# A four-layer sequence kernel: the expert group of four tiles placed second, the second chunk's first norms and sums on VectorE, and a new order table

## The chip, the core and the metric

The kernel runs on one core of one Trainium2 chip. The metric is the device time of one execution in microseconds (us). The kernel before was timed in nine runs: median 668.4, from 666.0 to 671.02.

A core has TensorE (PE in the profile; its weight loads are PEld), VectorE (DVE), ScalarE (ACT), GpSimd (POOL) and SyncE (SP, which only issues transfers). They run side by side and wait for each other through semaphores. Each engine works through its own queue strictly in order, so an instruction that waits holds up all that is queued behind it on its engine.

## The reference

The input is 8 sequences of 512 steps with 128 features, all float32. Four layers follow each other, each with a residual sum and a layer norm in front:

```python
x = x + ssm(layernorm(x))          # gated linear recurrence over the steps, both
                                   # outer weights divided by max(largest singular value, 1)
x = x + layernorm(x) @ W[idx] + b[idx]       # idx: argmax of logits + gumbel noise
x = x + delta(layernorm(x))        # 16 heads of 8; per step, with normalised k:
    # S = S + beta * (v - S k) k^T ;  o = S q        then  x + scan_out @ w_out + b_out
x = x + experts(layernorm(x))      # softmax router, the best 2 of 8 experts per token:
    # h = gelu(x w1[e]) (128 -> 512) ;  y = h w2[e] (512 -> 128) ;  weighted sum of the two
```

The third layer's state S of each sequence and head goes from step to step, so it is a chain over 512 steps.

## The kernel before

**Tiles and chunks.** A tile is 16 steps of all 8 sequences, 128 tokens. There are 32 tiles. They are worked in chunks of `SIZES` = 2, 4, 4, 4, 4, 4, 4, 4, 2 tiles; `FROM[g]` is a chunk's first tile. For each chunk the kernel runs `first_layers` (the first two layers: `scanned`, `ssm_out`, `linear`), then `delta_in` (projections, key norms and the 4x4 block matrices `tmat` of the delta rule), then `delta_rule`, then `route`.

**The recurrence.** `delta_rule` takes four steps at a time: each tile has 4 blocks, 128 in all. A block is six VectorE instructions, each of which needs the one before: a reduction of the last state product (`st<-so`), `prod<-tmat,st`, a reduction, `st<-kq,st`, a reduction, and the state product `so<-kq,st`. The last of these is called the state product below. GpSimd, TensorE and ScalarE turn the products of a tile into its output x3.

**The experts.** `route` norms x3, finds the two best experts and their weights, and appends its chunk to the open group. `GROUPS` (line 28) says which chunks share a group; when a group's last chunk is routed, `experts` is recorded for the whole group. It computes a place in a table in DRAM for each (token, expert) pair, such that each block of 128 rows belongs to one expert. GpSimd sends each tile's rows there with two indirect transfers (`scatter`, "places<-xne" in the profile, two for a tile). Then, block by block, SP loads the rows and the block's expert weights `w1b` (256 KB), TensorE transposes the rows, multiplies by w1 (`ph`), ScalarE takes the GELU (`hid`), TensorE multiplies by w2, and the results go to DRAM. Behind a group's last block GpSimd fetches the rows back (`back<-results`, again two for a tile), and they are weighted and summed into `fin` and written out. A group of n tiles has (2*128*n - 8)//128 + 8 blocks. The last chunk, of two tiles, is not sorted: `every_expert` runs all eight experts over it (called dense here).

**The start.** The largest singular value of two weight matrices comes from 21 squarings of each on TensorE, with copies on VectorE; at its end stands `gain`, which the first layer's output needs. The products of the expert weights with `less_last` (`kq<-in`) are spread in between.

**Who norms.** `factors` makes the scale and shift of a norm, `normalised` applies it tile by tile. With `leads` true the shift is one VectorE instruction and the norm a VectorE instruction for each tile; otherwise the shift is two GpSimd instructions and the norm a ScalarE instruction for each tile. `leads` is `g == 0`, the first chunk. In the same way `ssm_out` and `linear` sum on VectorE for the first chunk and for late chunks, and otherwise let TensorE add the residual through a product with the identity and ScalarE copy the sum.

**What sets the order.** Nothing is issued directly. A `Recorder` for each engine records every instruction into a `Plan` with its operands, a cost and a due time (`nc.key`, from `due(tile)` = 15 a tile). `Plan.ordered` then emits the recorded instructions in the order of the number table `ORDER` (line 383), and gives the PSUM banks from the string `BANKS` (line 630); both were made beforehand from the planner's own costs. So the position of each instruction in its engine's queue is written out by hand, as it were, in that table. As one helper issues all of them, nearly all lines of the profile name L330; groups are told apart by the names of their tiles.

**Lines the change touches:** 28 (`GROUPS`), 75 and 300 (`Plan`), 374 (`PRESUM` and the constants behind it), 383 (`ORDER`), 630 (`BANKS`), and in `seq_kernel` the functions `input_statistics`, `scanned`, `ssm_out`, `linear` and `scatter`.

Of the kernel before, what the change touches and what calls it, by code (L numbers as in the profile page):

```python
# [27 lines left out]
GROUPS = ((2,), (4, 4), (4, 4), (4, 4), (4,), (2,))  # L28
# [41 lines left out]
class Plan:  # L70
# [4 lines left out]
    def __init__(self, tc, banks):  # L75
        self.tc, self.hw, self.banks = tc, tc.nc, banks
        self.ops, self.seen, self.key, self.slack = [], {}, 0.0, 0.0
        self.tensor, self.vector, self.scalar, self.gpsimd, self.sync = (
            Recorder(self, e) for e in ("tensor", "vector", "scalar", "gpsimd", "sync")
        )  # L80
# [213 lines left out]
    def emit(self):  # L294
        kind = mybir.EngineType
        with self.tc.manual_schedule(engines={kind.PE, kind.DVE, kind.Activation, kind.SP}):
            for op, switch in self.best():
                if switch:
                    self.hw.scalar.preload_act_table_set(switch)  # L299
                made = op.emit()  # L300
                if op.engine == "gpsimd":
                    self.tc.keep_in_program_order(made)
# [51 lines left out]
def _cost(engine, name, n, kw):  # L354
# [16 lines left out]
TENSOR_SUMS = 12  # L371
PERIOD = 15.0
BEHIND = 8.0
BURST, WINDOW = 4, 6.0
LAG = {"tensor": 0.4, "vector": 0.3, "scalar": 0.3, "gpsimd": 0.3, "sync": 0.3}
# [8 lines left out]
    3, 10, 38, 43, 36, 37, 45, 35, 34, 48, 44, 1, 5, 53, 0, 9, 50, 49, 57, 46, 7, 335, 52, 8, 11, 32, 51, 47, 33, 4,  # L384
    12, 59, 126, 39, 61, 58, 31, 2, 13, 6, 16, 14, 327, 67, 62, 15, 40, 129, 63, 17, 64, 54, 130, 65, 18, 131, 336,
    66, 19, 343, 132, 21, 323, 133, 435, 55, 134, 324, 830, 135, 68, 153, 70, 145, 154, 328, 69, 146, 106, 444, 160,
    101, 107, 100, 325, 77, 152, 42, 147, 163, 60, 108, 326, 102, 155, 161, 390, 103, 391, 104, 392, 337, 148, 393,
    109, 344, 338, 156, 110, 112, 71, 149, 394, 87, 111, 41, 150, 98, 136, 157, 113, 151, 339, 367, 399, 158, 114,
    162, 340, 418, 137, 351, 159, 72, 165, 164, 400, 329, 375, 167, 341, 401, 330, 56, 397, 359, 405, 115, 74, 166,
    128, 395, 331, 116, 168, 406, 117, 22, 342, 332, 118, 176, 105, 170, 407, 119, 398, 169, 29, 171, 182, 175, 185,  # L390
    120, 333, 172, 138, 183, 173, 73, 174, 184, 334, 396, 187, 408, 402, 423, 188, 177, 409, 191, 139, 178, 403, 80,
    197, 179, 180, 181, 140, 99, 186, 141, 205, 346, 142, 192, 189, 410, 193, 404, 190, 345, 198, 199, 411, 194, 81,
    195, 200, 196, 204, 347, 206, 207, 201, 202, 209, 422, 203, 143, 412, 208, 210, 211, 348, 413, 213, 212, 214,
    219, 414, 446, 220, 215, 221, 226, 445, 222, 216, 349, 90, 415, 23, 223, 217, 224, 416, 218, 225, 417, 227, 447,
    229, 420, 228, 91, 231, 448, 419, 449, 424, 450, 230, 232, 144, 233, 421, 425, 236, 451, 235, 360, 237, 452, 241,
    427, 383, 238, 453, 249, 239, 234, 352, 240, 121, 243, 368, 250, 428, 458, 27, 20, 350, 253, 242, 460, 244, 254,
    429, 248, 258, 257, 245, 246, 251, 459, 247, 259, 263, 252, 271, 464, 260, 255, 261, 262, 272, 465, 256, 275,
    265, 454, 466, 276, 280, 281, 264, 455, 307, 426, 266, 282, 122, 279, 283, 270, 267, 284, 273, 268, 285, 269,
    293, 481, 274, 309, 277, 294, 297, 278, 286, 287, 298, 288, 301, 456, 292, 467, 289, 290, 291, 295, 362, 302,
    457, 361, 303, 468, 296, 461, 299, 88, 354, 300, 462, 353, 304, 384, 89, 469, 305, 25, 363, 313, 306, 355, 312,  # L400
    92, 376, 315, 463, 316, 24, 317, 318, 319, 320, 93, 470, 321, 364, 356, 430, 84, 322, 641, 431, 127, 432, 78,
    433, 28, 85, 434, 314, 365, 436, 30, 477, 437, 311, 471, 310, 308, 438, 79, 439, 440, 385, 94, 472, 123, 473, 95,
    124, 644, 82, 96, 125, 643, 645, 474, 441, 83, 442, 642, 475, 443, 499, 86, 482, 357, 358, 515, 517, 487, 516,
    518, 476, 519, 369, 522, 386, 521, 479, 523, 1065, 524, 478, 483, 520, 646, 525, 647, 484, 648, 649, 480, 783,
    650, 740, 377, 526, 378, 485, 527, 370, 486, 528, 379, 371, 655, 677, 488, 657, 489, 372, 490, 380, 373, 491,
    492, 656, 494, 651, 493, 387, 661, 388, 389, 653, 495, 662, 496, 652, 663, 366, 497, 664, 529, 97, 654, 26, 665,
    509, 659, 498, 658, 530, 666, 531, 660, 532, 500, 667, 501, 533, 502, 504, 534, 505, 503, 506, 535, 507, 1066,
    536, 508, 668, 381, 537, 548, 374, 547, 510, 538, 545, 511, 1068, 512, 546, 549, 669, 539, 513, 550, 540, 514,
    543, 695, 551, 541, 711, 552, 575, 1069, 576, 573, 670, 544, 578, 577, 554, 712, 574, 542, 714, 579, 553, 580,
    555, 558, 678, 671, 586, 581, 560, 382, 559, 557, 562, 672, 561, 563, 556, 582, 564, 673, 565, 592, 566, 583,  # L410
    567, 675, 568, 584, 569, 593, 585, 715, 594, 713, 595, 588, 674, 679, 596, 716, 590, 717, 597, 676, 589, 718,
    754, 680, 599, 587, 600, 719, 755, 682, 598, 720, 605, 601, 721, 681, 722, 591, 723, 602, 683, 724, 606, 725,
    603, 570, 614, 726, 1067, 684, 604, 571, 727, 685, 572, 728, 686, 729, 1070, 687, 619, 613, 730, 1071, 1413, 688,
    1072, 731, 1073, 607, 689, 617, 1074, 732, 690, 611, 733, 608, 734, 753, 735, 618, 691, 609, 615, 736, 692, 738,
    737, 610, 620, 739, 625, 757, 1136, 741, 616, 693, 758, 621, 694, 759, 696, 760, 622, 626, 697, 761, 612, 742,
    627, 699, 743, 1137, 762, 1079, 698, 629, 1135, 756, 623, 763, 624, 744, 628, 764, 1081, 745, 765, 1075, 766,
    1080, 630, 767, 1085, 746, 768, 1077, 631, 1086, 769, 1076, 1087, 747, 770, 771, 748, 772, 749, 632, 773, 1088,
    774, 700, 633, 701, 1078, 775, 702, 634, 703, 750, 1089, 776, 705, 777, 635, 778, 779, 636, 780, 781, 637, 1416,
    1138, 1090, 784, 1178, 1082, 751, 1139, 785, 752, 1140, 786, 1179, 1141, 1415, 1083, 787, 704, 1142, 1177, 1164,
    788, 1414, 1143, 706, 1417, 789, 707, 1084, 1144, 790, 708, 1145, 709, 1146, 1418, 1091, 1147, 791, 710, 1419,  # L420
    1148, 1102, 1149, 1150, 1420, 782, 999, 1092, 1151, 1000, 1152, 1119, 792, 1153, 1093, 793, 1154, 794, 1155,
# [217 lines left out]
def seq_kernel(  # L639
# [459 lines left out]
    def tiles_of(v):  # L1099
        return [v[:, i, :] for i in range(v.shape[1])]  # L1100
# [31 lines left out]
    def input_statistics(g, x):  # L1132
        of_input[g] = factors(moments(x, "i", 3), "i", 1, g == 0, NG)
# [887 lines left out]
```

## Time and profile before

| what | us |
|---|---|
| median of nine runs | 668.4 |
| the profiled execution | 670.72 |
| its span, first to last instruction | 669.0 |
| TensorE busy (80% of the span) | 532.7 |
| ScalarE busy (70%) | 468.8 |
| VectorE busy (69%) | 463.0 |
| GpSimd busy (69%) | 458.8 |
| end of the gain's computation on ScalarE | 51.4 |
| first block of the recurrence begins | 91.5 |
| last state product of tile 29 ends | 501.8 |
| last state product of tile 31 ends | 546.2 |
| last matmul ends | 662.9 |

Of the groups, these matter here (mean duration of one):

| group | count | mean ns |
|---|---|---|
| VectorE, six instructions of a block | 128 each | 491, 284, 291, 426, 497, 685 |
| GpSimd, rows to places | 60 | 1000 |
| GpSimd, rows back from results | 60 | 979 |
| ScalarE, table load | 64 | 1283 |
| ScalarE, GELU 128x512 | 111 | 597 |

A row of the profile has the line, engine and operation, then the tile written, an arrow, the tiles read, their shapes, the start and the duration, and in brackets how long the engine had been idle and who released it. TensorE's instructions are counted in passes: one float32 product shows as two. Some matmul records are missing from a trace, a few per cent.

### The profile page before, as it was taken

The numbers are of one execution on the slowest core, as the hardware profiler recorded it, in microseconds if no ns is written. First come the engines' busy times: TensorE is split into PE (matmuls) and PEld (weight loads), VectorE is DVE, ScalarE is ACT, GpSimd is POOL, SyncE is SP. The second block draws the span as 40 slices with busy tenths as digits, with TensorE's granted clock in tenths as the row PEclk, the third lists the DMA queues.
The fourth block names the chain that finished last, engine by engine and source line by source line (L and its number), as shares of the span: only waits on it lengthen the run. The fifth ranks groups of instructions, "written<-read, shape, count | busy, mean of one in ns | idle before, by whom it ended". The sixth has DMA issues, their size and how long they took to land.

```text
span 669.0 us, 10937 instructions
## 1 busy us (share of the span) xinstructions
PE 532.7 (80%) x3077; PEld 416.0 (62%) x3077; DVE 463.0 (69%) x1290; ACT 468.8 (70%) x984; POOL 458.8 (69%) x603
## 2 busy tenths in 40 slices
PE   3886668687796688796998787998978998778876
PEld 3653234454554455673676575787868987668775
DVE  7567158999988999989899998998971950002021
ACT  2875887879768579988999997857765553536421
POOL 6545467768768748899987978886589668454340
PEclk9898778989779789989999897999989988998988
DMA  4938145236243556446775585888887775665531
GB/s 133 326 116 271 59 107 148 68 80 157 64 126 77 167 138 181 135 123 193 198 196 155 146 218 151 232 224 202 217 218 230 220 228 191 188 211 186 168 106 35
DMA packets 96721, 110.16 MB, mean 165 GB/s; under 512 B 10179, under 2 KB 68206, under 8 KB 96662
## 3 DMA queue, kind: packets, MB, share of 16 engines
q1 hardware_dynamic: 91984, 101.31, 54.3%
q0 software_dynamic: 3904, 8.00, 4.4%
q8 instruction: 26, 0.43, 0.3%
q14 instruction: 33, 0.27, 0.1%
q10 hardware_dynamic: 774, 0.15, 0.1%
HBM read 85.90 MB, written 27.48 MB: 169 GB/s over the span
## 4 chain that ended last, share of the span: by engine, by line
DVE 34%; PE 30%; ACT 13%; POOL 9%; issue 5%; DMA 3%; another core or an unknown queue 3%; ACTq 1%; SPq 1%; DVEq 0%; POOLq 0%
DVE st L330 16%; PE in L330 11%; PE ph L330 9%; DVE so L330 7%; PE po L330 5%; POOL places L1685 4%; PE po L1747 4%; ACT f L330 3%; DVE prod L330 3%; ACT hid L330 2%; PE in L1747 2%; ACT L299 2%; ACT b L330 2%; POOL so L330 1%
## 5 line engine op out<-in xcount | busy, mean ns | idle before, releaser
L330 PE MATMUL ph<-xbT,w1b 128*128 128x128 f32 x760 | 142.6, 289 | 12.3 <-ACT hid L330 6.2
L330 PEld LDWEIGHTS ph<-xbT,w1b 128*128 128x128 f32 x760 | 115.0, 201 | 19.2 <-ACT hid L330 8.2
L330 ACT ACTIVATE hid<-ph 128x512 f32<-128x512 f32 x111 | 65.5, 597 | 86.6 <-PE ph L330 47.0
L1747 PE MATMUL po<-w_sb,hid 128*128 x536 | 105.5, 288 | 4.3 <-ACT hid L330 3.5
L1747 PEld LDWEIGHTS po<-w_sb,hid 128*128 128x128 f32 x536 | 85.6, 202 | 14.5 <-issue 8.4
L330 DVE TENSOR_TENSOR so<-kq,st 128x512 f32<-128x512 f32 x128 | 87.6, 685 | 5.8 <-PE in L330 0.6
L299 ACT ACT_TABLE_LOAD x64 | 82.1, 1283 | 9.2 <-DMA hid<-in_L_attn_ln_b_dram 8.1
L1685 POOL DMA_INDIRECT places<-xne,small_dest x60 | 60.0, 1000 | 20.7 <-issue 10.5
L330 POOL DMA_INDIRECT back<-results,small_dest x60 | 58.7, 979 | 21.3 <-issue 14.1
L330 DVE TENSOR_REDUCE st<-st 128x64 f32<-128x320 f32 x128 | 63.6, 497 | 3.7
L330 DVE TENSOR_REDUCE st<-so 128x32 f32<-128x320 f32 x128 | 62.8, 491 | 3.9 <-ACT so L330 0.8
L330 DVE TENSOR_TENSOR st<-kq,st 128x256 f32<-128x256 f32 x128 | 54.5, 426 | 3.5
L330 PE MATMUL po<-wo,so 128*128 128x128 f32 x240 | 48.6, 306 | 8.9 <-POOL so L330 6.6
L330 PEld LDWEIGHTS po<-wo,so 128*128 128x128 f32 x240 | 40.7, 215 | 23.9 <-POOL so L330 9.4
L330 PE MATMUL in<-b,wqkvb 128*128 128x512 f32 (+1 forms) x72 | 39.7, 641 | 11.5 <-ACT b L330 3.6
L1747 PE MATMUL in<-w_sb,hid 128*128 x224 | 45.6, 288 | 1.8 <-issue 1.3
L330 PE MATMUL in<-f,wT 128*128 128x512 f32 (+1 forms) x72 | 40.1, 650 | 8.1 <-DVE small_best L330 3.7
L330 DVE TENSOR_TENSOR prod<-tmat,st 128x128 f32<-128x128 f32 x128 | 36.4, 284 | 7.4 <-POOL tmat L330 4.2
L330 POOL TENSOR_TENSOR f<-f,f 128x512 f32<-128x512 f32 (+1 forms) x27 | 32.4, 1201 | 12.7 <-ACT f L330 12.5
L330 DVE TENSOR_REDUCE st<-prod 128x32 f32<-128x128 f32 x128 | 37.2, 291 | 5.6 <-ACT upd L330 1.0
L330 POOL TENSOR_TENSOR fin<-fin,back 128x512 f32<-128x512 f32 (+1 forms) x14 | 16.7, 1196 | 32.9 <-ACT back L330 32.7
L330 PE MATMUL ph<-ident,xb 128*128 128x128 f32 x95 | 28.3, 306 | 13.4 <-ACT hid L330 11.3
(339 smaller groups left out, 1389.6 us busy)
## 6 DMA issues: line engine op xcount, KB each, us to landing
kq<-scratch SPq DMA_DIRECT2D x64, 512.0 KB
w1b<-w1b_dram SPq DMA_DIRECT2D x103, 256.0 KB
xb<-places SPq DMA_DIRECT2D x20, 256.0 KB
results<-yb SPq DMA_DIRECT2D x20, 256.0 KB
places<-yb SPq DMA_DIRECT2D x2, 1472.0 KB
kq<-in_L_ffn_w_dram SPq DMA_DIRECT2D x2, 1024.0 KB
w1b_dram<-kq SPq DMA_DIRECT2D x2, 1024.0 KB
u_rows<-in_L_attn_u_dram SPq DMA_DIRECT2D x7, 256.0 KB
```

The lines of the kernel that those rows point to most:

```text
L299: self.hw.scalar.preload_act_table_set(switch)
L330: return method(*(on(x) for x in args), **{k: on(x) for k, x in kw.items()})
L1685: rows_out = hw.gpsimd.indirect_dma_start(out=table[0 : nblk * P, :], out_offset=bass.IndirectOffsetOnAxis(ap=at, axis=0), in_=src, in_off ...
L1747: return hw.tensor.matmul(out_.on(nc.banks), lhsT=src, rhs=w2_f[:, bass.ds(at + c * P, P)], start=(c == 0), stop=(c == NHB - 1),)
```

## The change

Three things, and a fourth that the numbers leave without effect:

1. The groups are 2; 4; 4, 4; 4, 4; 4, 4; 2 tiles and not 2; 4, 4; 4, 4; 4, 4; 4; 2. The chunk sizes stay. The group of four tiles is now tiles 2 to 5; the last recorded group is tiles 22 to 29, where it was 26 to 29.
2. The second chunk (four tiles) is led as the first: its first and second norms' shifts and norms and its two residual sums go to VectorE. The transposed input of both chunks is copied out of PSUM by VectorE.
3. `ORDER` and `BANKS` are new throughout.
4. The plan can make a row transfer wait for an earlier one when `ROW` of them stand in a row without a longer GpSimd instruction between them; `ROW` is 99.

```diff
-GROUPS = ((2,), (4, 4), (4, 4), (4, 4), (4,), (2,))
+GROUPS = ((2,), (4,), (4, 4), (4, 4), (4, 4), (2,))
...
+                self.to_land = self.row[-1] if op.by_rows and len(self.row) == ROW else None
                 made = op.emit()
-                if op.engine == "gpsimd":
-                    self.tc.keep_in_program_order(made)
+                if op.engine != "gpsimd":
+                    continue
+                self.tc.keep_in_program_order(made)
+                if self.to_land:
+                    wait = mybir.DependencyInfo(mybir.DependencyClass.Sync, mybir.DependencyReason.DATA)
+                    self.tc.add_manual_dep(made.ins, self.to_land, wait, reason="short rows of indirect transfers")
+                    self.row = []
+                if op.by_rows:
+                    self.row.append(made.ins.name)
+                elif op.cost > 0.6:
+                    self.row = []
...
+LEADS = 2
 BURST, WINDOW = 4, 6.0
+ROW = 99
...
 ORDER = (
...
 BANKS = (
...
     def input_statistics(g, x):
-        of_input[g] = factors(moments(x, "i", 3), "i", 1, g == 0, NG)
+        of_input[g] = factors(moments(x, "i", 3), "i", 1, g < LEADS, NG)
...
-        nc.scalar.copy(xT, transposed(normalised(x, rstd, shift, tiles_of(xn.rearrange("p (i d) -> p i d", d=D)), leads=g == 0)))
+        copied = nc.vector.tensor_copy if g < LEADS else nc.scalar.copy
+        copied(xT, transposed(normalised(x, rstd, shift, tiles_of(xn.rearrange("p (i d) -> p i d", d=D)), leads=g < LEADS)))
...
     def ssm_out(x, r, g):
-        if g == 0 or FROM[g] > TENSOR_SUMS:
+        if g < LEADS or FROM[g] > TENSOR_SUMS:
             nc.vector.scalar_tensor_tensor(x1, tokens_out(r, wT[:, 4, :]), gain, x, ALU.mult, ALU.add)
...
     def linear(x1, g):
-        leads = g == 0
+        leads = g < LEADS
...
-        if g == 0 or FROM[g] > TENSOR_SUMS:
+        if g < LEADS or FROM[g] > TENSOR_SUMS:
             nc.vector.tensor_add(x2, tokens_out(xT, wsel), x1)
...
                 for before_ in scattered:
-                    tc.declare_no_dep(rows_out.ins, before_, reason="every row has places of its own")
+                    if before_ != nc.to_land:
+                        tc.declare_no_dep(rows_out.ins, before_, reason="every row has places of its own")
```

One rule of `experts` depends on a group's last tile: where the group ends at tile 28 or later, its rows are weighted and summed by VectorE multiply-adds, one for each tile and expert (now two chunks, before one), and otherwise by ScalarE multiplications and GpSimd sums.

## Prediction

> **What bounds the kernel now.** I read the page's slices first, then a table of stretches cut at the stage limits, then VectorE's timeline around the recurrence's end, then ScalarE's and VectorE's timelines of the start. The slices (40, of 16.7 us) show three stages.
>
> ```profile
> PE   3886668687796688796998787998978998778876
> DVE  7567158999988999989899998998971950002021
> ACT  2875887879768579988999997857765553536421
> POOL 6545467768768748899987978886589668454340
> ```
>
> A start of five slices in which no engine is full all through; a middle, to about 500 us, in which VectorE is at 9; and a tail in which VectorE is idle and TensorE is the fullest. The second view is the table of stretches (start:end, length, busy us and instruction counts of TensorE, weight loads, VectorE, ScalarE, GpSimd, then TensorE's clock, DMA share, GB/s). I cut at the gain's arrival (51.4), the first recurrence block (91.5), the end of tile 29 (501.8), the last state product (546.2) and the last matmul (662.9).
>
> ```profile
> 0.00:51.40 51.40, 36.48 (x157) 26.74 (x157) 33.78 (x154) 32.19 (x92) 26.81 (x64) 0.93 0.62 191
> 51.40:91.50 40.10, 27.09 (x74) 14.67 (x74) 14.73 (x29) 29.59 (x66) 22.15 (x37) 0.75 0.48 153
> 91.50:501.80 410.30, 332.58 (x1853) 247.72 (x1852) 374.14 (x983) 332.62 (x675) 322.40 (x405) 0.91 0.60 158
> 501.80:546.20 44.40, 40.02 (x305) 37.65 (x305) 24.84 (x78) 23.43 (x52) 34.81 (x44) 0.92 0.79 224
> 546.20:662.90 116.70, 96.52 (x694) 89.16 (x693) 14.86 (x49) 50.98 (x103) 52.67 (x55) 0.94 0.55 166
> 662.90:669.00 6.10, 0.00 (x0) 0.00 (x0) 0.61 (x2) 0.00 (x0) 0.00 (x0) 0.72 0.08 22
> ```
>
> VectorE works 374 of 410 us in the middle. From 501.8 to 662.9, 161.1 us, TensorE works 136.5 us and is idle 24.6. So the time is start + VectorE's middle + TensorE's tail. Third, VectorE as tile 30 begins:
>
> ```profile
> 501.91 0.49 DVE L330 TENSOR_REDUCE st<-so 128x32 f32<-128x320 f32 x1
> 508.22 0.29 DVE L330 TENSOR_TENSOR x<-po,base 128x128 f32<-128x128 f32 x1 [5.81 <-PE po L330]
> ...
> 514.11 0.69 DVE L330 TENSOR_TENSOR acc<-po,x 128x512 f32<-128x512 f32 x1 [0.99 <-issue]
> 518.59 0.29 DVE L330 TENSOR_TENSOR prod<-tmat,st 128x128 f32<-128x128 f32 x1 [3.79 <-POOL tmat L330]
> ```
>
> The recurrence stands still from 502.4 to 518.6, because the block matrices (tmat) of the last chunk come from GpSimd, which was sending 16 row scatters. TensorE meanwhile was 90% busy, so this hole looks large and costs little.
>
> **The expert group moved.** A group of n tiles has (2·128n - 8)//128 + 8 blocks: 11, 15 and 23 for 2, 4 and 8 tiles. Six groups give 95 routed blocks before and after; no matmul goes away there. I counted the order tables behind the last state product of tile 29: 521 matmuls and transposes before, 524 after. Behind that of tile 31: 357 before, 413 after. So the last recorded group grows from 15 blocks to 23, but the plan has the same TensorE work left at the end of tile 29. What differs is where the recurrence stands: in the new order the last chunk's tmat is written at tile 29.25, before tile 30 needs it, where it stood at 29.75 behind the last of the scatters. The 16.2 us hole goes, and tiles 30 and 31 should take about 2 x 14.5 us (their VectorE rows sum to 29.0) and not 44.4. TensorE then has 56 more instructions after the recurrence, 56 x 2 passes x 0.131 us (40.02/305, the saturated stretch) = 14.7 us. Gain 15.4, loss 14.7: nothing is won by the hole itself. That is the main step of this forecast.
>
> Two things are late next. The last group's 16 scatters: the order has them from tile 31.25 on, with 427 TensorE instructions left at the first and 342 at the last, and the first of its transposes at 317. Their spacing in the trace was 1.4 us (550.89, 552.31, 553.76, 555.23): 22.7 us for 16, which 85 x 2 x 0.131 = 22.3 us of TensorE work covers. Then the landing, 5.2 us, and the block load, 3.0 us in the chain of waits; 25 instructions cover 6.6 of these 8.2. And the gathers behind the last block: 16 where there were 8, with 8 more VectorE multiply-adds (0.35 us each) in place of 8 ScalarE multiplications and 2 GpSimd additions. Gathers followed each other by 1.25 us (636.34 to 645.21): 10 us more. Before, the last block's copy ended at 632.2, the gathers began at 636.3, the last multiply-add ended at 651.1. After: 632.2 + 4.1 + 20.1 + 4.9 = 661.3 on the old scale, then two output hops begun 2.3 us apart, some 5 us: 666. The old end was 669, through the dense experts, so this stays hidden by 3 us. If that cover is gone it costs what it exceeds.
>
> **The start.** ScalarE loses 12 instructions of the second chunk: eight norms at 0.49, three copies of 512 at 0.59 and the first chunk's 0.36 copy, 6.0 us. TensorE loses two products with the identity. VectorE gets 8 norms (0.35), copies and sums of 0.68 to 0.74, two shifts at 0.16, GpSimd loses four small ones at 0.2. VectorE is busy only 14.7 of 40.1 us there, which is the cover; without it the price would be about 6 us. One wait is new: the second chunk's x2 sum (0.68) with its two moments (0.42 each) stands in VectorE's queue between block 0's first reduction and the first chunk's tmat; all of block 0 is queued behind it. Before, the two moments alone stood in front of that reduction; I count the 0.7 us in the lower bound below. Between the gain and the copy that lets block 0 begin, ScalarE's queue holds 64 instructions, 34.8 us with two table loads, before, and 50, 27.5 us, after; the copy stood at 91.25. The timeline shows what is in front of the first chunk's keys:
>
> ```profile
> 67.57 0.56 ACT L330 ACTIVATE b<-in,cols 128x256 f32<-128x256 f32 x1 [0.78 <-PE in L330]
> ...
> 74.60 1.28 ACT L299 ACT_TABLE_LOAD   x1
> ...
> 77.88 1.28 ACT L299 ACT_TABLE_LOAD   x1
> ...
> 79.81 0.46 ACT L330 ACTIVATE knq<-in,cols 128x256 f32<-128x256 f32 x1
> ```
>
> Seventeen instructions of 10.9 us stand between b and knq, eight of 7.0 us in the new order. Upper bound of the gain: 7.3 us. Lower bound below nothing: two more weight products and ten more VectorE instructions (3.6 us) now stand ahead of the gain; TensorE was 95% busy from 30 to 40 us, and if nothing of the 7.3 is won and most of this delays the squarings, the start is 3 us later. I take 4 us earlier, nearer the upper end, because VectorE was idle 17.6 of the first 51.4 us.
>
> The norms have one bad price in the trace:
>
> ```profile
> 61.58 0.33 DVE L330 TENSOR_SCALAR b<-x,small_rstdb,small_shiftb 128x128 f32<-128x128 f32 x1
> 61.83 2.51 DVE L330 TENSOR_SCALAR base<-x,small_rstdb,small_shiftb 128x128 f32<-128x128 f32 x2
> ```
>
> The same instruction takes 0.33 us and, beside GpSimd's two products of 1.30 and 1.26 us from 61.72 on, 1.26 each. Eight norms lie between 8 x 0.35 = 2.8 and 8 x 1.29 = 10.3 us; I take the lower, as four stand ahead of the gain, where GpSimd is busy 26.8 of 51.4 us, and the rest has 25 us of idle VectorE.
>
> The Trainium skill, "SBUF — State Buffer", Who interferes with whom, has the rule behind this row and against this part of the change: a VectorE tensor_scalar in a two-port mode and a GpSimd instruction take a shared port pair in turn, and the second blocks fully. By the rule the worst case is the 10.3 us, by the low row 2.8; GpSimd would be held up by the same ports.
>
> In the middle, from block 0 to the end of tile 29, VectorE's rows sum to 392.2 us in the old order and 393.3 in the new: +1.1. Table loads fall from 64 to 56, 8 x 1.28 = 10.3 us of ScalarE, which is not the bound there; in the tail a load delays a GELU that TensorE waits for. The Trainium skill, "ScalarE: Activation LUTs", What ACT_TABLE_LOAD costs, prices a switch at 2.66 us with its drain; here the next instruction starts 1.30 us after the load does (74.60, 75.90), and by the page's price the eight would be 21 us.
>
> SP's 338 recorded transfers stay 338: each block takes its weight load and row loads along, and DMA engines at 0.55 to 0.79 in the tail have room for six to eight blocks more behind 546. The code for rows (ROW = 99) does nothing: no run of row transfers reaches 99.
>
> **Sum.** End of tile 29: 501.8 - 4 + 1.1 = 498.9. TensorE's tail: 161.1 x 524/521 = 162.0, less 3 of the 24.6 idle us for loads and for scatter waits that a deeper store of blocks covers (bounds: 0 and 14, the idle beyond 9% as at 501.8 to 546.2). Then 6.1 us of output. 664.0 of span, 5.0 less than 669.0. The profiled execution took 670.7, 0.3% over the median of 668.4; I put the difference to the median: 663.4 us.
>
> **Rivals.** *Scatters too late* (slower). With groups of eight tiles the way from the last tile's end to the first product of its rows took 69.5 us before (tile 25 ends at 446.4, blocks of it at 515.95). The new order hopes for some 54 (30 for tile 30 and 31, 16 of scatters left, 8 of landing). With L us of it the end is T29 + L + 317 x 0.309 (161.1/521 per instruction) + 6.1; it decides from L = 61. At 69.5: 498.9 + 69.5 + 98.0 + 6.1 = 672.5, and 675.6 where the start brings 1 us: some 674, or 673.4 as a time. For: GpSimd's rows behind the recurrence sum to 59.7 us, and the block load has 1.6 us less cover than it takes; against: the blocks of the group before cover.
> *Nothing moves.* The start's 4 us are lost in the middle, where the second and third chunks wait for GpSimd (80% busy): 669, time 668.4. For: tile 0 took 20.0 us (91.5 to 111.5), VectorE idle for 3.7 of them.
> *A full tail.* With 56 more instructions stored TensorE keeps the pace of 501.8 to 546.2 (44.4 us for 164 instructions, 0.271): 498.9 + 142.0 + 6.1 = 647. I take half of the way from 664, 655.5, as GELU waits came back in every slice after 546: time 655.
>
> **How the numbers follow.** Forecast 0.38, scatters too late 0.31, nothing 0.17, full tail 0.14. 0.3% (2 us) is about what this measurement tells from no change. Faster by more: the full tail, most of the forecast (0.33), little of nothing moves (0.03), 0.50; slower: the late scatters (0.30) and a part of nothing moves (0.06), 0.36; the same 0.14. The forecast's own range is 658 to 669; 8 in 10 reach from 651 to 679, the late scatters with a start 3 us later.
>
> **What would show it.** Right: block 0 before 89 us; no wait of VectorE over 4 us at tile 30, the last state product near 528; TensorE over 87% busy from there to its end; tmat of the last chunk ahead of the scatters. Wrong: TensorE idle over 4 us before the last group's first transposes (late scatters); the gain after 54 us; a last multiply-add of the gathered rows behind the last dense product.

## The result, and the profile after

The changed kernel takes 684.85 us (median of 20 runs, 675.65 to 689.86) against 667.13 us (62 runs of the kernel before on the same chips): a ratio of 1.0237, with a 95% interval of 1.0211 to 1.0264. The change costs 2.4%, where 0.7% of gain was forecast, and the time lies above the predicted range. Medians here are of all runs, ratios of the fast ones alone (six of the 20 runs of the changed kernel count as slow), so that this ratio is below the quotient of the medians, 1.0265.

The profiled execution took 682.29 us, 680.6 of them the span. Its first lines and the slices (40, of 17.0 us; busy tenths):

```profile
span 680.6 us, 10891 instructions
...
PE 530.6 (78%) x3073; PEld 415.2 (61%) x3073; DVE 477.7 (70%) x1312; ACT 453.8 (67%) x956; POOL 454.4 (67%) x597
...
PE   3986868668586788888878878994977968979964
...
DVE  7685459899999999989998898996797800001112
```

TensorE's busy time is about what it was (530.6 us, before 532.7), so the 11.6 us that the span grew are TensorE standing idle. VectorE is busy to slice 32, with dips to 6 and 7 in slices 28 and 29; the hole of the old kernel, the 1 in its slice 31, is gone.

The table of stretches, cut at the same events as in the prediction (start:end, length, busy us and counts of TensorE, weight loads, VectorE, ScalarE, GpSimd, then TensorE's clock, DMA share, GB/s): the gain's arrival, block 0, the end of tile 29, the last state product, the last matmul.

```profile
0.00:52.00 52.00, 37.58 (x155) 27.28 (x155) 40.23 (x155) 27.40 (x76) 26.02 (x64) 0.93 0.56 168
52.00:90.90 38.90, 27.78 (x68) 13.27 (x68) 16.61 (x39) 27.01 (x61) 18.61 (x25) 0.69 0.50 166
90.90:511.80 420.90, 329.67 (x1857) 250.88 (x1857) 380.60 (x986) 327.28 (x677) 327.68 (x423) 0.91 0.59 157
511.80:545.60 33.80, 29.47 (x217) 27.25 (x216) 26.84 (x82) 19.09 (x38) 22.68 (x26) 0.90 0.68 191
545.60:674.00 128.40, 106.08 (x785) 96.47 (x783) 13.46 (x53) 53.02 (x105) 59.42 (x62) 0.97 0.58 170
674.00:680.60 6.60, 0.00 (x0) 0.00 (x0) 0.00 (x0) 0.00 (x0) 0.00 (x0) 0.77 0.27 61
```

(The first cut is at 52.0; the gain itself came at 57.5. The last is at 674.0; the last matmul ended at 673.0.) Set against the rows before, TensorE's idle time is length minus busy: 14.9 and 13.0 us in the two stretches of the start before, 14.4 and 11.1 now; 77.7 before and **91.2** now in the middle; 4.4 and 4.3 in the stretch of tiles 30 and 31; 20.2 and 21.3 in the tail, up to the last matmul. So 13.5 us of idle time are new in the middle, before any of the work that the change moved to the end begins. From the end of tile 29 on, TensorE has 1002 records left and the kernel needs 168.8 us; before it was 999 records and 167.2 us.

The same in phases of the recurrence, by which the experiments are compared below (us, one execution each):

| | start to tile 0's end | tiles 1-26 | 27-29 | 30, 31 | rest | span |
|---|---|---|---|---|---|---|
| before | 111.5 | 349.3 | 40.9 | 44.4 | 122.8 | 669.0 |
| after | 113.5 | 352.2 | 46.1 | 33.9 | 135.0 | 680.6 |

The hole of tile 30 did close: 10.5 us. The rest behind the recurrence grew by 12.2. And tiles 27 to 29 hold a new hole. VectorE's timeline at tile 27 of the changed kernel (start, us, engine, line, operation, tiles and shapes, idle time before and who ended it):

```profile
470.62 0.43 DVE L341 TENSOR_TENSOR st<-kq,st 128x256 f32<-128x256 f32 x1
480.49 0.29 DVE L341 TENSOR_TENSOR x<-po,base 128x128 f32<-128x128 f32 x1 [9.45 <-PE po L341]
480.70 0.49 DVE L341 TENSOR_REDUCE st<-st 128x64 f32<-128x320 f32 x1
```

The recurrence stands in the middle of a block for 9.45 us, because a residual sum (`x<-po`) stands in VectorE's queue and waits for TensorE. What TensorE waited for is in its own timeline, and what that waited for is in GpSimd's:

```profile
475.66 0.80 PE L341 MATMUL po<-wo,so 128*128 128x128 f32 x2 [6.84 <-POOL so L341]
```

```profile
460.65 0.26 POOL L341 TENSOR_TENSOR small_both<-small_mine 128x32 f32<-128x32 f32 x1
461.07 0.99 POOL L1699 DMA_INDIRECT places<-xne,small_dest  x1 [0.17 <-issue]
462.37 0.96 POOL L1699 DMA_INDIRECT places<-xne,small_dest  x1 [0.30 <-issue]
...
472.48 0.96 POOL L1699 DMA_INDIRECT places<-xne,small_dest  x1 [0.30 <-issue]
473.47 0.92 POOL L341 TENSOR_TENSOR qkp<-qkp,upd 128x384 f32<-128x384 f32 x1
474.34 1.26 POOL L341 TENSOR_TENSOR so<-so 128x512 f32<-128x512 f32 x1
```

Ten scatters follow each other, one each 1.27 us, and the two sums for the attention output (`qkp`, `so`) of tile 26 come behind all of them. In the order table they stand behind the second of the ten. The table isn't what runs: the plan pins each GpSimd instruction behind the one issued before it, but a scatter declares that it depends on no earlier scatter of its group, and with that declaration the pin between two scatters goes as well. A scatter whose predecessor in the table is a scatter may then go ahead of other work. Compared place by place with the queue of the same kernel with its scatters pinned (experiments 11 and 1 below), 30 of GpSimd's 603 instructions are others in the kernel before, and 45 of 597 in the changed one.

### The profile page after: what moved, and what is told of

It is laid out like the page before. It is cut to its first block, busy times and chain, and to the rows that moved or that the text cites. A ratio compares the mean times of both kernels' runs of the same rounds, so it can differ in the third digit from the quotient of the medians.

```text
span 680.6 us, 10891 instructions
## 1 busy us (share of the span) xinstructions
PE 530.6 (78%) x3073; PEld 415.2 (61%) x3073; DVE 477.7 (70%) x1312; ACT 453.8 (67%) x956; POOL 454.4 (67%) x597
## 4 chain that ended last, share of the span: by engine, by line
DVE 35%; PE 25%; POOL 14%; ACT 12%; issue 9%; another core or an unknown queue 2%; DMA 2%; DVEq 0%; POOLq 0%; ACTq 0%
DVE st L341 16%; PE in L341 9%; PE ph L341 6%; DVE so L341 6%; PE po L341 6%; POOL places L1699 5%; ACT f L341 4%; DVE prod L341 3%; PE po L1762 2%; ACT L300 2%; POOL so L341 2%; POOL back L341 1%; ACT b L341 1%; ACT hid L341 1%
## 5 line engine op out<-in xcount | busy, mean ns | idle before, releaser
L341 PE MATMUL ph<-xbT,w1b 128*128 128x128 f32 x760 | 141.2, 290 | 21.3 <-ACT hid L341 15.5
L341 PEld LDWEIGHTS ph<-xbT,w1b 128*128 128x128 f32 x760 | 114.8, 202 | 33.8 <-ACT hid L341 18.0
L1762 PE MATMUL po<-w_sb,hid 128*128 x496 | 96.2, 283 | 3.4 <-DVE so L341 2.3
L1762 PEld LDWEIGHTS po<-w_sb,hid 128*128 128x128 f32 x496 | 77.6, 197 | 10.1 <-issue 8.1
L1699 POOL DMA_INDIRECT places<-xne,small_dest x60 | 60.6, 1011 | 16.3 <-issue 12.2
L341 PE MATMUL po<-wo,so 128*128 128x128 f32 x248 | 50.0, 316 | 16.8 <-POOL so L341 12.2
L1762 PE MATMUL in<-w_sb,hid 128*128 x264 | 55.5, 300 | 4.9 <-DVE acc L341 2.7
L341 PEld LDWEIGHTS po<-wo,so 128*128 128x128 f32 x248 | 42.5, 224 | 26.9 <-POOL so L341 14.1
L341 DVE TENSOR_TENSOR st<-kq,st 128x256 f32<-128x256 f32 x128 | 54.5, 426 | 3.5
L1762 PEld LDWEIGHTS in<-w_sb,hid 128*128 128x128 f32 x264 | 43.7, 209 | 9.3 <-DVE acc L341 2.9
L341 PE MATMUL in<-f,wT 128*128 128x512 f32 (+1 forms) x72 | 41.7, 667 | 8.9 <-ACT f L341 6.9
L341 POOL TENSOR_TENSOR qkp<-qkp,upd 128x384 f32<-128x384 f32 x32 | 29.2, 913 | 21.3 <-ACT upd L341 18.5
L341 POOL TENSOR_TENSOR f<-f,f 128x512 f32<-128x512 f32 (+1 forms) x27 | 31.1, 1153 | 17.0 <-ACT f L341 16.8
```

The source lines that it names most:

```text
L341: return method(*(on(x) for x in args), **{k: on(x) for k, x in kw.items()})
L1699: rows_out = hw.gpsimd.indirect_dma_start(out=table[0 : nblk * P, :], out_offset=bass.IndirectOffsetOnAxis(ap=at, axis=0), in_=src, in_off ...
L1762: return hw.tensor.matmul(out_.on(nc.banks), lhsT=src, rhs=w2_f[:, bass.ds(at + c * P, P)], start=(c == 0), stop=(c == NHB - 1),)
```

## The experiments

The kernel before was timed beside each experiment, 665.7 to 666.7 us (median); ratios are to it.

**1. The rows in their places.** In the plan's `emit`, each scatter or gather is also held behind the last other GpSimd instruction, and each other instruction behind the rows since:

```diff
+            last, rows = [], []
...
                 self.tc.keep_in_program_order(made)
+                held = mybir.DependencyInfo(mybir.DependencyClass.NoSync, mybir.DependencyReason.DATA)
+                for name in last if op.by_rows else rows:
+                    self.tc.add_manual_dep(made.ins, name, held, reason="the table's order")
+                if op.by_rows:
+                    rows.append(made.ins.name)
+                else:
+                    last, rows = [made.ins.name], []
```

> The changed kernel, with one addition: each row scatter on GpSimd is tied behind the last arithmetic instruction that stands before it in the order table (and the next arithmetic one behind all scatters before it), so that runs of ten scatters no longer go ahead of the presum of tile 27. Nothing is left out. Theory A (the stalls of the recurrence made the change slow): tile 27 takes 13 to 14 us and not 21.7, tile 29 ends at 503 to 504 and not 511.8, and the end follows by the same 8 us: time near 677 us, ratio to before about 1.014. Theory B (TensorE's work behind tile 29 sets the end, the stall is hidden): tile 29 ends as early, but the time stays at 683 to 686 us, ratio 1.023 to 1.026.

Measured: 677.96 us, 1.0182 [1.0141, 1.0223]. The stall shrinks from 9.45 to 1.82 us, as VectorE's timeline of this kernel shows:

```profile
472.68 0.29 DVE L349 TENSOR_TENSOR x<-po,base 128x128 f32<-128x128 f32 x1 [1.82 <-PE ph L349]
```

The tile takes 14.1 us and not 21.7, tile 29 ends at 506.5 and not 511.8. In the profiled execution the end hardly moves: the rest behind the recurrence takes 139.6 us in place of 135.0, with the same 785 TensorE records. But that execution, 681.5 us, was the slowest of the seven. By the medians of all runs the pins bring 6.9 us, by the ratios 0.55%, and the two ratios' intervals just meet; how much of the stall comes through to the end isn't settled by this. What is: the stall is real and is not, alone, what the change costs.

**2 and 3. The start alone, the group alone.** The first has the groups and the order of the kernel before with the new start (`LEADS = 2`, the table of after up to block 0, then that of before); the second the groups and the order of after with the start of before (`LEADS = 1`, the first chunk's copy back on ScalarE).

> The groups of before and its order behind the first recurrence block, with the new start alone: second chunk's norms and sums on VectorE and the changed kernel's order up to the first block. My forecast's step (start 4 us earlier): block 0 at 87.5 us, time near 663 us, ratio 0.994. Rival, read from the changed kernel's trace (block 0 only 0.6 us earlier and tile 0 2.6 us longer): tile 0 ends 2 us later, time 667 to 669.5 us, ratio 1.000 to 1.003. If the start were what made the change slow: 675 us or more, ratio 1.012 and up.

> The changed kernel's groups and its order behind the first recurrence block, with the start of before: second chunk's norms and sums on ScalarE and TensorE again, in before's order. If the group's move and the table behind it hold the whole loss: 682 to 687 us, ratio 1.022 to 1.029. If half of the loss lay in the start: 675 to 678 us, ratio 1.012 to 1.016.

Measured: 1.0036 [1.0001, 1.0071] and 1.0318 [1.0273, 1.0363]. The start brings nothing; the group and its order carry all of the loss, and a little more. The second table is a splice of two, so the 0.8% by which it is worse than the whole change isn't read as a gain of the start.

**4 and 6. Could the old hole have been closed without the group?** Both have the groups of before, the pins of experiment 1, and the last chunk's tmat chain set ahead of the scatters in the table; the second also sets the `so` sum ahead and everything of tiles 30 and 31 115 places earlier.

> The kernel before, with the last chunk's block matrices (tmat: fifteen GpSimd instructions with the two head sums and their copies) moved ahead of the last ten scatters and two additions, and the scatters tied to their places. The recurrence's hole at tile 30 (502.4 to 518.6 us) should go: last state product at 530 to 532 us and not 546.2. Theory B, the main step of the forecast (TensorE's work sets the end, the hole is worth nothing): time 665 to 669 us, ratio 0.997 to 1.003. Theory A (the recurrence sets the end): 15 us of it come through, or at least half: 652 to 660 us, ratio 0.978 to 0.989.

> The kernel before once more with its hole at tile 30 taken out, now in all queues: the last chunk's tmat ahead of the scatters, tile 29's sums ahead of the seven scatters left, and all steps of tiles 30 and 31 some 115 places earlier in the order, the additions that wait for TensorE behind them. The last state product should come at 528 to 533 us and not 546.2, with 408 TensorE instructions behind it and not 357. Theory B (main step of the forecast, by the formula 531 + 408 x 0.32 + 6.3 = 668): time 664 to 669 us, ratio 0.996 to 1.004. Theory A (the recurrence alone sets the end): 650 to 657 us, ratio 0.976 to 0.986.

Measured: 1.0127 [1.0076, 1.0178] and 1.0318 [1.0285, 1.0352]. Both lie outside what either theory allowed. VectorE no longer waits for tmat; it waits for TensorE's sums in its place. In the first:

```profile
511.26 0.29 DVE L338 TENSOR_TENSOR x<-po,base 128x128 f32<-128x128 f32 x1 [11.51 <-PE po L338]
```

In the second:

```profile
514.73 0.29 DVE L338 TENSOR_TENSOR x<-po,base 128x128 f32<-128x128 f32 x1 [6.45 <-PE ph L338]
...
528.65 0.69 DVE L338 TENSOR_TENSOR acc<-po,x 128x512 f32<-128x512 f32 x1 [6.04 <-remote]
```

Tile 30 still takes 30.5 and 28.9 us, and tiles 30 and 31 together 54.5 and 40.7 (before 44.4); in the second the rest behind them grows to 146.7 us (before 122.8). (The profile names no releaser that it knows for the last wait shown.) What hid behind the wait for tmat was, in experiment 4, one for TensorE of 11.5 us. Whether a better table could close it at a gain isn't shown.

**7 and 8. The group without a hand-made table.** `ORDER = ()` in both, so that the planner makes the order by its costs; 7 with the groups of before, 8 with the new ones and the old start, both with the pins.

> The kernel before without its written order: the planner in the program makes the order from its own costs, and the scatters are tied to their places. It serves as the base for the next run. 466 TensorE instructions stand behind the last state product in this order (362 in the written one, counted with register loads). Expected slower than before: 675 to 700 us.

> The same planner's order for the changed groups, with the start of before (second chunk on ScalarE): only the place of the four-tile group differs from the run before. 424 TensorE instructions behind the last state product. If the group's place as such costs time (a last recorded group of 23 blocks for 15): 10 to 18 us over the planned order of before. If the loss comes from the written table and not from the group: within 5 us of it, or faster.

Measured: 791.53 us (1.1886 [1.1845, 1.1927]) and 808.04 us (1.2132 [1.2093, 1.2172]). Both are far slower than was expected of experiment 7 (675 to 700 us). Without either table the new groups cost 16.5 us, 2.1%, about as much as with them. But the loss lies elsewhere: tiles 1 to 26 take 449.6 us in experiment 8 and 433.3 in 7, and the rest behind the recurrence 160.6 and 160.9. So the pair shows that the new groups cost time in another order as well, and not that they cost it by the same way.

**5, 9, 10. One suspect shortened at a time.** Each leaves work of the changed kernel out, by numbers of the record that aren't emitted: blocks 16 to 22 of the last recorded group (63 TensorE instructions); 8 of its last 16 scatters; the last 8 gathers with their sums.

```diff
+            if 4413 <= number <= 4505 and not 4426 <= number <= 4431:
+                continue
```

> The changed kernel without blocks 16 to 22 of its last recorded group (tiles 22 to 29): 63 TensorE instructions, seven GELUs, seven weight loads, two row loads and two stores are left out, so 16 blocks remain where the kernel before has 15 there; the rows of these blocks are not computed. The first five runs fit one formula: end = end of tile 31 + TensorE instructions left there x 0.32 us + 6.3 us. Theory B (the tail's length is TensorE's instructions left): end of tile 31 unchanged at 544 to 547 us, span 660 to 664, time 662 to 668 us, ratio 0.995 to 1.003. Rival (something else sets the tail, the 16 gathers and their additions or the scatters): time 674 to 681 us, ratio 1.012 to 1.021.

> The changed kernel without the last eight of the sixteen row scatters of its last recorded group; the rows they carry are not delivered, so the group's block loads can begin some 11 us sooner. All TensorE work stays. Rival of the forecast (scatters too late: the first product of the last group's rows waits for them, 66.8 us behind tile 29's end in the changed kernel): the end moves by 7 to 11 us, time 674 to 678 us, ratio 1.011 to 1.017. If TensorE's backlog of earlier blocks (71 of 72 GELUs done when the rows arrive) covers the wait: time 682 to 686 us, ratio 1.020 to 1.027.

> The changed kernel without the last eight of its sixteen final gathers and without the eight multiply-adds behind them (tiles 26 to 29 are written without their routed part). My forecast's step (the eight more gathers stay hidden behind the dense experts): 683 to 686 us, ratio 1.021 to 1.026. If they set the end: 5 to 10 us less, 675 to 680 us, ratio 1.011 to 1.018.

Measured: 1.0162 [1.012, 1.0204], 1.025 [1.0221, 1.0279], 1.0273 [1.0241, 1.0305]. The blocks are worth 0.75%, 5 us, a quarter of what 63 x 0.31 us would be; scatters and gathers nothing. So no one of the three ends the time alone.

**11. The rows in their places, in the kernel before.**

> The kernel before with its row scatters tied to their places in the order table, as the changed kernel had it in the first run of this study. No stall of the recurrence stands behind a run of scatters there before tile 30 (largest wait of VectorE from 120 to 500 us: 1.9 us). Expected: no difference, 665 to 669 us, ratio 0.997 to 1.003. If scatters out of place cost time wherever they stand: 661 to 664 us, ratio 0.991 to 0.996.

Measured: 664.31 us, 0.997 [0.9943, 0.9997]. The misplaced instructions of the old kernel cost about 2 us. This is the best complete version that the study has; it is ahead of the kernel before by about as much as can be told. It is also the fair partner of experiment 1: with the scatters pinned in both, the change still costs 1.0182/0.997, 2.1%, or 13.7 us by the medians. Of the 16.8 us between the two profiled executions 7.0 lie before the end of tile 29 and 9.8 behind it, where tiles 30 and 31 take 10.8 us less and the rest 20.5 more.

**12 to 18. Removals together.** With the pins: all three shortened (12), the blocks alone (13), blocks and gathers (14), blocks and scatters (15). Without the pins: all three (16), blocks and gathers (17), blocks and scatters (18).

> The changed kernel with its scatters tied to their places, without blocks 16 to 22 of the last recorded group, without eight of its row scatters and without eight of its final gathers and their multiply-adds: what remains behind tile 31 has the size that it has in the kernel before (16 blocks for 15, eight scatters, eight gathers). If the larger last group and the one stall are the whole loss: 664 to 670 us, ratio 0.996 to 1.006. If a part lies elsewhere, in VectorE's longer rows up to tile 29 (374 to 381 us busy): 672 to 677 us, ratio 1.009 to 1.016.

> The changed kernel with its scatters tied to their places and without blocks 16 to 22 of the last recorded group. If the two gains simply add (0.6% and 0.8%): 670 to 674 us, ratio 1.007 to 1.012. If each alone was covered by the other: 658 to 666 us, ratio 0.988 to 1.000, as with all four parts.

> As the run before, and without the last eight final gathers and their multiply-adds. If the gathers end last once the blocks are fewer: 5 to 10 us less than the run before, down to 658 to 664 us, ratio 0.988 to 0.997. If not: within 2 us of it.

> As the run before the last one (scatters in place, fewer blocks), and without eight of the last group's sixteen row scatters. If the rows' arrival decides once TensorE has less behind it: 6 to 11 us less, ratio 0.988 to 0.998. If not: within 2 us of it.

> The changed kernel without blocks 16 to 22, without eight of the last scatters and without the last eight gathers and their multiply-adds, its scatters not tied (with the stall of 9 us at tile 27). If the recurrence's stall comes through to the end once the tail is short: 664 to 669 us, 6 to 9 us more than the 658 of the same kernel with scatters in place. If it is hidden: 656 to 660 us.

> The changed kernel without blocks 16 to 22 and without the last eight final gathers and their multiply-adds; scatters as they stand, not tied. If the sixteen scatters hold it back: 675 to 680 us, as with the blocks alone (ratio 1.013 to 1.020). If the gathers do: 662 to 668 us, ratio 0.994 to 1.003.

> The changed kernel without blocks 16 to 22 and without eight of the last group's sixteen row scatters; scatters not tied. If the scatters hold it back: 662 to 668 us, ratio 0.994 to 1.003. If the gathers do: 675 to 680 us, ratio 1.013 to 1.020.

| left out | rows as they run | rows pinned |
|---|---|---|
| nothing | 1.0237 [1.0211, 1.0264] | 1.0182 [1.0141, 1.0223] |
| blocks | 1.0162 [1.0120, 1.0204] | **0.9889** [0.9854, 0.9924] |
| blocks, gathers | 1.0084 [1.0046, 1.0123] | 0.9857 [0.9807, 0.9907] |
| blocks, scatters | 0.9998 [0.9962, 1.0033] | 0.9864 [0.9824, 0.9904] |
| all three | 0.9969 [0.9940, 0.9999] | 0.9875 [0.9828, 0.9921] |

Read along the first two rows. Pins alone bring 0.55%, blocks alone 0.75% (by the medians of all runs about 1.0% each), both together 3.5%. Once the rows are pinned, the 63 TensorE instructions are worth 1.0182 - 0.9889 = 2.9%, 19.5 us or 0.31 us each, which is the 0.309 that the prediction used for an instruction of the tail. With the pins, nothing is gained by fewer scatters or gathers as well: TensorE's backlog ends the time. Without them, fewer scatters bring 1.6% as soon as the blocks are out, and fewer gathers 0.8% (experiment 17, between its two expectations). So the changed kernel has two ways to its end, nearly equally long: one is TensorE's backlog behind the recurrence; the other is shortened by pins and by fewer scatters and gathers. Taking one away leaves the other.

Three things this table doesn't show. The pins put every misplaced instruction back, and not only those of tile 27: of the 20.9 us between the profiled executions of experiments 5 and 13, tiles 27 to 29 hold 5.8, and the rest is spread from the start (2.0) to the tail (7.5). What the second way consists of is open: that the last group's rows come late was the expectation, but in the trace of experiment 5 TensorE's long waits before those rows, 6.30 and 3.08 us, both follow pauses of ScalarE (6.81 and 3.82 us) whose releaser the profile doesn't know. And the 63 instructions weren't taken out of the kernel before, which has as much TensorE work left at the end of tile 29; that the larger last group makes the backlog longer than it was is therefore argued, and not shown.

The tail of experiment 13 beside that of the changed kernel (from the last state product to the last matmul, within 1 us):

```profile
533.20:647.50 114.30, 92.54 (x666) 83.10 (x664) 13.35 (x53) 47.02 (x94) 59.40 (x62) 0.97 0.58 167
```

119 records fewer than 785, and 14.1 us less than 128.4; the scatters, gathers and their sums on GpSimd (59.40 us, x62) are the same to the instruction.

The middle's phases show what the pins do, and what they don't:

| | tiles 1-26 | 27-29 |
|---|---|---|
| after, experiments 3, 5, 9, 10, 16 to 18 (rows as they run) | 351.0 to 355.7 | 45.9 to 46.9 |
| experiments 1, 12 to 15 (pinned) | 348.3 to 354.3 | 40.7 to 41.4 |
| before, experiments 4, 6, 11 (old groups) | 347.0 to 350.4 | 39.0 to 42.6 |

In tiles 27 to 29 the first set doesn't meet the others: the stall costs the changed order 5 us wherever its rows run out of place, and none where they are pinned. In tiles 1 to 26 the first set (mean 352.8) lies wholly above the third (348.9), while the pinned ones (350.1) reach into both. So some 4 us seem to be lost there as well; no experiment says by what.

## Why the prediction was wrong, step by step

**The step that failed: "End of tile 29: 501.8 − 4 + 1.1 = 498.9".** It was 511.8, 12.9 us later than forecast and 10.0 later than before. The other part of the sum, from there to the end, was forecast at 165.1 us and took 168.8. By terms:

- *"I take 4 us earlier."* It was 0.6 us (block 0 at 90.91, before 91.5). The shorter queue of ScalarE is there: from the gain to block 0 it took 33.4 us, before 40.6: 7.2 less, where 7.3 was the forecast's upper end. But the gain itself came at 57.5 and not at 50.9. The two rows (lists of one tile's instructions: durations, first and last start) of before and after:

```profile
L330 DVE TENSOR_REDUCE gain<-sp x1: 154/154/154, 50.9 to 50.9; 128x1 f32<-128x2 f32 x1
```

```profile
L341 DVE TENSOR_REDUCE gain<-sp x1: 155/155/155, 57.5 to 57.5; 128x1 f32<-128x2 f32 x1
```

  The lower bound named this way of failing and allowed it 3 us; VectorE worked 8.57 and 8.12 us of the two stretches from 30 to 50 us, where it had worked 5.88 and 6.37. Two small rows of the gain's own chain also stood beside GpSimd products, 1.06 and 1.28 us where 0.17 is usual. The size is not steady: the same start came to its gain at 52.3 to 57.9 us and to block 0 at 84.1 to 91.7 in the other executions, the old one at 49.1 to 50.9 and 89.3 to 91.5. Experiment 2 says that it is worth nothing: 1.0036. The norms were priced right by the low row: the eight of the second chunk took 3.18 us in the changed kernel, where 2.8 were taken and 10.3 was the upper bound.
- *"From block 0 to the end of tile 29 ... +1.1."* It was +10.6: 2.6 in tile 0 (22.6 us, before 20.0; one scan took 2.29 us, before 1.72, where most of its kind take 1.23), 2.9 in tiles 1 to 26, 5.2 in tiles 27 to 29. The last is the stall, and it is the one term that the experiments settle (1, 12 to 15). VectorE worked 6.5 us longer in this stretch (380.60 us, before 374.14) and stood idle for the other 4.1. The sum of rows took it that what stands in the order table is what runs. The kernel's instructions as built, and not the table, have the ten scatters ahead of the `so` sum.
- *"The 16.2 us hole goes"*, and tiles 30 and 31 take "about 2 x 14.5". The hole went, with one wait of 3.87 us left and 33.8 us in place of 29.0. That "nothing is won by the hole itself" was right: 10.5 us won, 12.2 us paid behind it, for 91 more records at 127.3/785 = 0.162 us each, 14.8 us; 14.7 were forecast.
- TensorE's tail, *"less 3 of the 24.6 idle us"*. Nothing of it came: from the end of tile 29 to the last matmul TensorE stood idle for 25.6 us, and the stretch took 161.2 us where 159.0 were forecast. With 1.5 us more of output behind that matmul (7.6, before 6.1) this makes the 3.7 us by which the second part of the sum was missed.
- The old hole was read as a wait for tmat, which it was, but not alone: with tmat early, experiment 4 still waits there for 11.5 us, for TensorE.

**Same work, later end.** That "the plan has the same TensorE work left at the end of tile 29" is confirmed (999 and 1002 records). In this pair of executions the end of the kernel follows the end of tile 29, 168.8 us behind it and 167.2 before. It need not: in its profiled execution experiment 1 moved the end of tile 29 forward by 5.3 us and the end of the span by 0.8. In the stretches of the trace TensorE falls behind between 450 and 525 us. Before:

```profile
450.00:475.00 25.00, 22.39 (x173) 20.04 (x172) 22.21 (x73) 18.81 (x41) 13.66 (x23) 1.00 0.89 219
475.00:500.00 25.00, 19.12 (x139) 17.90 (x139) 22.12 (x56) 15.54 (x30) 20.92 (x22) 0.93 0.83 215
500.00:525.00 25.00, 22.91 (x173) 21.08 (x172) 8.97 (x21) 14.36 (x32) 21.70 (x30) 0.93 0.77 220
```

After:

```profile
450.00:475.00 25.00, 15.81 (x107) 13.56 (x106) 20.35 (x54) 13.48 (x28) 19.75 (x23) 0.82 0.71 207
475.00:500.00 25.00, 22.75 (x161) 21.07 (x161) 18.04 (x41) 13.72 (x32) 13.00 (x18) 0.91 0.69 197
500.00:525.00 25.00, 17.86 (x122) 15.90 (x122) 19.73 (x62) 12.87 (x23) 16.18 (x26) 0.91 0.69 189
```

Up to 450 us the two are level (5 records of 1761 apart); in the three stretches to 525 the changed kernel falls 95 behind. With the smaller group as the last but one, the old kernel had TensorE work for these stretches, and the hole of tile 30 gave it time; the new one gets those blocks later, when the recurrence that would have covered them has ended. That last sentence is a reading of counts; what the runs show is the table of removals above. That the rest of experiment 1 takes 4.6 us more than that of the changed kernel for the same records is of the size by which executions differ: in experiment 3, whose rows run as in the changed kernel, it took 138.9 us.

**The rivals.** *Scatters too late* came nearest: it forecast a time of 673.4 to 674, and its condition held, the first transposes of the last group's rows being copied at 578.6, 66.8 us behind tile 29 (it decides from 61). Yet TensorE was idle for no more than 1.85 us before them, as the blocks of the group before lasted until then, and experiment 9 took half of those scatters out and gained nothing. Only with the blocks out and the rows unpinned do the scatters cost time (experiment 18 against 5), and there too no wait for the rows themselves was found. *Nothing moves* was right of the start and wrong of the rest. *A full tail* fell: TensorE was 83% busy after 545.6.

**The signs named.** "Block 0 before 89 us": no. "No wait over 4 us at tile 30": yes (3.87). "The last state product near 528": no, 545.6. "TensorE over 87% busy": 87.2% in tiles 30 and 31, not after. "Tmat of the last chunk ahead of the scatters": yes. "The gain after 54 us" was named as a sign of error, and came. The gathers stayed hidden as forecast, by 1.2 us where 3 were expected (last multiply-add 671.85, last dense sum 673.0).

## What to carry to other kernels

An order written into a table is a wish: compare what each engine runs with it before summing rows, above all where instructions declare that they don't depend on each other. A hole in the bounding engine can be the cover under which another engine does its work; closing it moves that work behind the hole, and pays only where the other engine has room there (10.5 us won and 12.2 lost here). And where two ways to the end are nearly equally long, taking each away alone shows little: 0.55% and 0.75% here, 3.5% together. Removals show what a piece of work is worth in one order; that the change made it cost more takes the same removal in the kernel before.

## What the runs showed of the hardware

**Some small VectorE rows stand until a running GpSimd product ends.** VectorE in the changed kernel:

```profile
334.95 0.29 DVE L341 TENSOR_TENSOR prod<-tmat,st 128x128 f32<-128x128 f32 x1
335.15 1.63 DVE L341 SCALAR_TENSOR_TENSOR small_place<-small_starts,small_place 128x64 f32<-128x64 f32 x1
336.70 0.28 DVE L341 TENSOR_REDUCE st<-prod 128x32 f32<-128x128 f32 x1
```

GpSimd beside it:

```profile
334.35 2.35 POOL L341 TENSOR_TENSOR both<-both,f 128x1024 f32<-128x1024 f32 x1
```

`small_place` ends at 336.78 and GpSimd's product at 336.70; the recurrence's next row waits behind it. The recurrence's own rows, such as `prod` at 334.95, run at full speed beside the same product. The Trainium skill, "SBUF — State Buffer", Who interferes with whom, has this: an instruction of VectorE with two inputs in SBUF contends with a GpSimd instruction that reads SBUF, and one with at most one SBUF input, outside the two-port modes, doesn't. The recurrence's state `st` lies in PSUM, `small_place` reads both inputs from SBUF; the trace agrees. Two kinds of rows with one tensor as input were lengthened as well, `small_where` (TENSOR_SCALAR, 1.30 us at 539.72, else 0.16) and `small_dest` (CAST, 1.01 us at 343.58, else 0.18); in which mode they ran the profile doesn't say. From tile 1 to tile 31, 19 rows took over 0.3 us more than the shortest row with the same tiles and shape in their trace, 14.1 us in all; before, 14 rows 9.0 us. That a new order costs by such meetings was seen in rows, and not tried by an experiment of its own.

**A pause of ScalarE that no queue explains.** The copy of an expert's result after the recurrence starts late in all kernels with the new groups that were looked at, 3.95 us in the changed kernel, 4.49 in experiment 1 and 4.38 in experiment 13, though its input was ready 2 us earlier or more:

```profile
551.72 0.59 ACT L341 COPY yb<-in 128x512 f32<-128x512 f32 x1 [3.95 <-remote]
```

The profile names no releaser that it knows. A transfer in a queue of the kind "instruction" moves between 547 and 548 us, as the pause begins at 547.8; whether that is the cause stays open. ScalarE pauses without a known releaser at other rows too, and did in the kernel before (5.77 us before a GELU at 648.01).
